# Two groups of x loads moved behind the first softmaxes of a Perceiver kernel

## The chip, the cores and the metric

The kernel runs on one core of one Trainium2 chip. The metric is the time on the device in microseconds (us), the median of several executions. Names used below: PE is TensorE, where "PEld" is its loading of weights; DVE is VectorE; ACT is ScalarE; POOL is GpSimd; SP is SyncE, which issues nearly all DMAs here. Each engine works through a queue of its own in order, and semaphores tie the queues together.

## The reference

A two-layer Perceiver step on x of 64 x 32 rows by 256 features, in float32. Each layer has cross attention into a context, self attention and a feed-forward part, each on a layer norm of x and added to x. The change lies in the first of the six, the cross attention of layer 0:

```python
def _L0_xattn_ref(q, latent_kv, Wq, Wkv_expand, Wout):      # 16 heads of 16
    qp = q @ Wq.T
    k, v = jnp.split(latent_kv @ Wkv_expand.T, 2, axis=-1)
    ...                                                     # split into heads
    scores = jnp.einsum('bhqd,bhkd->bhqk', qh, kh) * inv_sqrt_d
    scores = jnp.where(causal, scores, jnp.finfo(scores.dtype).min)
    attn = jax.nn.softmax(scores, axis=-1)
    out = jnp.einsum('bhqk,bhkd->bhqd', attn, vh)
    return out.transpose(0, 2, 1, 3).reshape(b, sq, H) @ Wout.T

x = x + _L0_xattn_ref(_layernorm(x, axis=-1), ctx_512, L0_xattn_Wq, L0_xattn_Wkv_expand, L0_xattn_Wout)
```

The causal mask lets 32 rows of a batch element see only its first 32 context rows, so only those are used here.

## The kernel before

The 2048 rows of x are 16 tiles of 128 rows (`NT`), `xs[0]` to `xs[15]`, which stay in SBUF through all six parts; four tiles make a group (`NG` = 4). A tile of x is 128 KB.

**Loads.** The program first issues all loads of its start on SP's queue: x of group 0 (L75), constants (L77), the weights `a_q` and `a_kv` (L86 to L96), the context of group 0 (`load_ctxa(0)`, L100 and L101), `a_o` (L105) and `vec` (L107); then x of the three other groups, twelve loads (L109), the context of groups 1 to 3, the rest of the constants (L112), and weights for later (L367, L372) with some tables (`cosN`, `sinN`, L669).

**The cross attention of layer 0** works by tiles in a software pipeline. For a group: `ln_group` or `norm` makes the layer norm, in the parts `stats` (L161, L162, DVE: BATCH_NORM_STATS2 and BATCH_NORM_AGGREGATE, each tile by itself), `ln_scale` for the whole group (POOL adds eps and raises to the power -1/2, L148 and L149; DVE makes the shift `lnh`, L176), and `ln_out` (L187, DVE, `xn_a`). `group(g, part)` turns the normalised rows (part 0, L226 and L230), makes the queries (part 1, L391 and L394) and the keys (part 2, L397; ACT spreads them into `kda`, L405).

For a tile: `score(t)` is 2 x 32 small matmuls into the PSUM tile `S_a` (L294), of which there is one; `softmax_rows` takes it out on DVE with scale and mask (`s_a`, L245), finds the maximum (`mx_a`, L254) and subtracts it on POOL (L255); `power(t)` is the exponential on ACT (L420); `share(t)` sums on DVE (`su_a`, L425), inverts (`ri_a`, L427) and multiplies on POOL (L428). `values(t)` makes the values on PE (`va`, L439) and masks them on DVE into `vda` (L449, four instructions). `heads_on_partitions(t)` turns the probabilities on PE (`ptp_a`, L263) and copies them on ACT (L265); `gather(t)` multiplies them with the values (`oa`, L464), and `project(t)` multiplies with `a_o` (`ya`, L493) and adds to x on DVE (L496). A step t of the loop holds, in this order on PE: the scores of t + 1, the projection of t - 2, the values of t + 1, the transpose of t, the gathering of t - 1, one part of the next group, and then the layer norm's part for the group after that (`norm(t // 4 + 2, t % 4, ...)`). Ahead of the loop, group 0 is normalised and made into queries and keys, tile 0 gets its scores, values and softmax, and group 1 is normalised.

**What sets the order.** PE's order is the order in which the program is written (a manual schedule). The queues of the other engines are filled by the tile framework's scheduler, which may move an instruction ahead of others once its operands can be there; loads on SP keep their order. So the order on DVE is not that of the text: in the built program DVE's instructions for the layer norm of groups 2 and 3 (written in the loop) stand ahead of the first tile's `s_a`.

**A column as a sign.** The kernel already holds back loads of weights for the next part (L482 to L487): POOL copies one column of a fresh result into the tile that is to be loaded, and the load, which overwrites it, must wait for that copy.

Of the kernel before, what the change touches and what calls it, by code (L numbers as in the profile page):

```python
# [13 lines left out]
P = 128  # L14
B, S, D = 64, 32, 256
NT = B * S // P
# [21 lines left out]
def bc(ap, axis, n):  # L38

    shape = list(ap.shape)  # L40
    shape.insert(axis, n)
    return ap.unsqueeze(axis).to_broadcast(shape)
# [3 lines left out]
def perceiver_kernel(ctx: ExitStack, tc: tile.TileContext, a: dict, out: bass.AP):  # L46
    nc = tc.nc
# [19 lines left out]
    def sm(name, shape):  # L67
        return small.tile(shape, F32, tag=name.split("_")[0], name=name)
# [4 lines left out]
    xs = [x[:, :D] for x in xf]  # L73
# [24 lines left out]
    def load_ctxa(g):  # L98
        src_ = a["ctxa"].rearrange("d (t c) -> d t c", c=P)[:, 4 * g : 4 * g + 4, :]
        nc.sync.dma_start(ctxa[0:DC, 4 * g : 4 * g + 4, :], src_)  # L100
        nc.sync.dma_start(ctxa[DC:P, 4 * g : 4 * g + 4, 0:64], src_[:, :, 64:P])  # L101
# [3 lines left out]
    nc.sync.dma_start(a_o, a["a_woT"].rearrange("(k p) o -> p k o", p=P))  # L105
    vec = const.tile([P, V_N], F32, name="vec")
    nc.sync.dma_start(vec, a["vecs"])  # L107
    for t in range(4, NT):
        nc.sync.dma_start(xs[t], a["x"][t * P : (t + 1) * P, :])  # L109
    for g in range(1, NG):  # L110
        load_ctxa(g)
    nc.sync.dma_start(cst[:, C_COST:], a["consts"][:, C_COST:])  # L112

    ident = cst[:, C_ID : C_ID + P]
# [244 lines left out]
    with tc.tile_pool(name="wA", bufs=2) as work, tc.tile_pool(  # L359
# [62 lines left out]
        def share(t):  # L422
            s = sc[t]
            su = sm(f"su_a{t}", [P, NH])
            nc.vector.tensor_reduce(su, s, AX.X, ALU.add)  # L425
            ri = sm(f"ri_a{t}", [P, NH])
            nc.vector.reciprocal(ri, su)  # L427
            nc.gpsimd.tensor_tensor(s, s, bc(ri, 2, S), ALU.mult)  # L428

        def values(t):  # L430

            vd = vals[t] = work.tile([P, 4, 4, 4, NH], F32, tag="vd", name=f"vda{t}", bufs=3)

            v_ps = [ps2.tile([P, 512], F32, tag="mm", name=f"va{t}_{z}") for z in range(2)]
            for jj in range(2):
                for z in range(2):
                    zs = slice(64 * z, 64 * z + 64)
                    for r in range(4):
                        nc.tensor.matmul(  # L439
                            v_ps[z][32 * r : 32 * r + 32, jj * D : (jj + 1) * D],  # L440
                            ctxa[zs, t, jj * S : (jj + 1) * S],
                            a_kv[zs, D : 2 * D],
                            start=True,
                            stop=True,
                            tile_position=(64 * z, 32 * r),
                        )
            for z in range(2):
                for jj in range(2):
                    nc.vector.tensor_tensor(  # L449
                        vd[:, 2 * z + jj],  # L450
                        v_ps[z][:, jj * D : (jj + 1) * D].rearrange(
                            "p (c h d) -> p c h d", c=4, h=4
                        ),
                        bc(bc(m4, 2, 16), 1, 4),
                        ALU.mult,
                    )
# [51 lines left out]
        values(0)  # L508
        power(0)
        share(0)  # L510
        lat[1] = ln_group(1, "a", power=True)

# [7 lines left out]
        for t in range(NT + 2):  # L520


            if t + 1 < NT:
                score(t + 1)
            if t > 1:
                project(t - 2)
            if t + 1 < NT:
                values(t + 1)
            if t < NT:
                turned[t] = heads_on_partitions(sc.pop(t), ps1, t, work, "a")  # L530
            if t + 1 < NT:
                power(t + 1)
            if 1 <= t <= NT:
                gather(t - 1)
            group(t // 4 + 1, (2, 0, 1, 3)[t % 4])
            norm(t // 4 + 2, t % 4, "a", mvs, lat)
            if t + 1 < NT:
                share(t + 1)
            for step in first.get(t, ()):
                step()  # L540
# [171 lines left out]
    with tc.tile_pool(name="wB", bufs=2) as work, tc.tile_pool(  # L712
# [237 lines left out]
        for t in range(NT + 1):  # L950
# [28 lines left out]
            if t < NT:  # L979
                share(t)  # L980
# [1054 lines left out]
```

## Time and profile before

| | us |
|---|---|
| median of 3 runs | 1284.66 |
| lowest and highest | 1284.02 and 1288.3 |
| profiled execution | 1288.21 |
| its span | 1286.4 |

Busy times of the profiled execution, out of its span:

| engine | busy us | share |
|---|---|---|
| PE | 1185.0 | 92% |
| PEld | 830.2 | 65% |
| DVE | 771.1 | 60% |
| ACT | 554.5 | 43% |
| POOL | 367.4 | 29% |

The mean granted clock of TensorE over the span was 0.941 of full speed. In a row of the timeline the first number is the start in us from the span's start, the second the length; then engine, line, operation, output<-input; in brackets stands how long the engine was idle before it and what ended that. A row that merges several instructions ends in their number (x4), and its length covers them all. "xcount" rows of stages give for each engine its busy time and in parentheses the number of instructions. A busy PE is not PE at its peak: its matmuls overlap.

### The profile page before, as it was taken

To read this page: it belongs to the slowest core of one execution; us is meant where nothing else is said; L and a number is where in the kernel's file an instruction comes from. 1 tells how busy PE (TensorE), PEld (TensorE's weight loads), DVE (VectorE), ACT (ScalarE), POOL (GpSimd) and SP (SyncE) were. 2 spreads that over 40 slices of the span, in tenths; PEclk is the share of its full clock that TensorE was granted. 3 is DMA by queue.
4 is the path that set the end of the run, shared out by engine and by line. 5 is a ranking of instruction groups with operands and counts; after the bars stand their busy time and mean duration, and the time that the engine had idled before them with its cause. 6 is when DMAs were issued, how large, how long until landed. Compare 5 with 4: busy or idle time off the path is not lost. (4 is left out here: it accounts for less than half of the span.)

```text
span 1286.4 us, 26074 instructions
## 1 busy us (share of the span) xinstructions
PE 1185.0 (92%) x10173; PEld 830.2 (65%) x10173; DVE 771.1 (60%) x1801; ACT 554.5 (43%) x1297; POOL 367.4 (29%) x438
## 2 busy tenths in 40 slices
PE   6999999999999998999889999999998798569997
PEld 4556767777776565776757667767765466436664
DVE  5666247778768875443287878776774564434333
ACT  2337354464544641213355646565564464311111
POOL 2333243455433621000154252010011354411111
PEclk8789999999999999989989989999999897669999
DMA  5021122343242423902263353111100344011110
GB/s 150 19 78 42 28 75 67 108 140 98 83 141 71 135 89 103 274 10 68 55 158 104 63 141 104 47 36 47 36 1 2 133 152 149 18 38 42 44 39 18
DMA packets 94971, 103.08 MB, mean 80 GB/s; under 512 B 37792, under 2 KB 71329, under 8 KB 94626
## 3 DMA queue, kind: packets, MB, share of 16 engines
q1 hardware_dynamic: 92978, 97.19, 26.4%
q0 software_dynamic: 1872, 4.23, 0.9%
q8 instruction: 81, 1.33, 0.4%
q14 instruction: 40, 0.33, 0.1%
HBM read 69.45 MB, written 32.85 MB: 80 GB/s over the span
## 5 line engine op out<-in xcount | busy, mean ns | idle before, releaser
L1348 ACT ACTIVATE pp<-Sd,nm 128x257 f32<-128x257 f32 x256 | 118.0, 474 | 77.1 <-DVE nm L1344 72.5
L761 PE MATMUL qb<-xT_b,b_q 128*128 128x256 f32 x512 | 123.4, 390 | 0.0
L761 PEld LDWEIGHTS qb<-xT_b,b_q 128*128 128x128 f32 x512 | 96.4, 193 | 39.9 <-issue 19.8
L852 PE MATMUL yb<-b_o,oTb 128*128 128x256 f32 x512 | 115.1, 384 | 0.0
L852 PEld LDWEIGHTS yb<-b_o,oTb 128*128 128x128 f32 x512 | 97.6, 192 | 14.0 <-issue 1.0
L1357 DVE TENSOR_TENSOR pp<-pp,rd 128x514 f32<-128x514 f32 x128 | 100.9, 789 | 2.1
L1344 DVE TENSOR_REDUCE nm<-Sd 128x2 f32<-128x514 f32 x128 | 82.9, 684 | 19.7 <-PE Sd L1336 19.6
L1379 ACT COPY pTd<-pt 128x512 f32<-128x512 f32 x112 | 61.5, 599 | 54.7 <-PE pt L1373 54.7
L1396 PE MATMUL od<-pTd,na 128*64 128x256 f32 x480 | 67.0, 401 | 11.2 <-issue 9.9
L780 POOL TENSOR_TENSOR q2b<-qTb 128x512 f32<-128x512 f32 x64 | 65.5, 1051 | 28.3 <-ACT qTb L769 17.0
L1336 PE MATMUL Sd<-ct,qTd 64*128 64x257 f32 x480 | 68.9, 404 | 0.7 <-ACT pp L1348 0.7
L769 ACT COPY qTb<-qb 128x512 f32<-128x512 f32 x64 | 37.4, 584 | 72.4 <-PE qb L761 70.8
L1373 PE MATMUL pt<-cst,pp 128*128 128x128 f32 x512 | 66.9, 274 | 0.0
L871 POOL TENSOR_TENSOR ynb<-ynb,vec 128x256 f32<-128x256 f32 x16 | 11.6, 724 | 188.4 <-DVE ynb L870 188.4
L1373 PEld LDWEIGHTS pt<-cst,pp 128*128 128x128 f32 x512 | 58.9, 141 | 9.8 <-issue 5.4
L1134 PE MATMUL qd<-xT_d,d_m 128*128 128x256 f32 x256 | 64.1, 393 | 0.2 <-ACT xT_d L230 0.2
L814 DVE RECIPROCAL rqb<-rqb 128x512 f32<-128x512 f32 x16 | 53.5, 3342 | 17.8 <-ACT rqb L809 17.8
L1412 PE MATMUL yd<-d_n,co 128*128 128x256 f32 x256 | 63.2, 403 | 0.0
L643 PE MATMUL yc<-c,hc 128*128 128x256 f32 x256 | 59.2, 387 | 2.7 <-DVE hc L638 2.7
L1910 POOL DMA_INDIRECT out_dram<-os,ti x23 | 22.6, 984 | 126.0 <-DVE os L1907 103.1
L1412 PEld LDWEIGHTS yd<-d_n,co 128*128 128x128 f32 x256 | 50.0, 200 | 13.4 <-issue 6.5
L1134 PEld LDWEIGHTS qd<-xT_d,d_m 128*128 128x128 f32 x256 | 46.6, 191 | 16.9 <-issue 6.4
(371 smaller groups left out, 2376.6 us busy)
## 6 DMA issues: line engine op xcount, KB each, us to landing
srt<-pad SPq DMA_DIRECT2D x17, 1040.0 KB
mb<-maskd SPq DMA_DIRECT2D x64, 128.0 KB
ct<-ctd SPq DMA_DIRECT2D x30, 257.0 KB
rct<-in_ctxT_dram SPq DMA_DIRECT2D x32, 128.5 KB
rrt<-in_ctxT_dram SPq DMA_DIRECT2D x64, 64.2 KB
ctd<-rct SPq DMA_DIRECT2D x32, 128.5 KB
nad<-rna SPq DMA_DIRECT2D x16, 256.0 KB
fw<-in_f_wg_dram SPq DMA_DIRECT2D x8, 512.0 KB
```

The costliest lines, as they stand in the source:

```text
L761: nc.tensor.matmul(q_ps[:, hh, :], b_q[:, k, h * P : (h + 1) * P], xT[:, k, c0 : c0 + 256], start=(k == 0), stop=(k == KC - 1),)
L780: nc.gpsimd.tensor_tensor(q2[:, 4 * h4 : 4 * h4 + 4, :], q, q, ALU.mult)
L852: nc.tensor.matmul(y_ps, oT[:, h, :], b_o[:, h, :], start=(h == 0), stop=(h == NH - 1))
L1134: nc.tensor.matmul(q_ps[:, r, :], m[:, k, pr * P : (pr + 1) * P], xT[:, k, c0 : c0 + 256], start=(k == 0), stop=(k == KC - 1),)
L1336: nc.tensor.matmul(s_ps[:, hh, :NKV], qT[hs, b % 8, 4 * u : 4 * u + 4, :], ct[hs, b % 4, :], start=True, stop=True,)
L1344: nc.vector.tensor_reduce(nm, s_ps[:, :, :NKV], AX.X, ALU.max, negate=True)
L1348: nc.scalar.activation(pp[:, hh, :], s_ps[:, hh, :NKV], AF.Exp, bias=nm[:, hh : hh + 1], accum_out=sd[:, hh : hh + 1],)
L1357: nc.vector.tensor_tensor(pp, pp, bc(rd, 2, NKV), ALU.mult)
L1373: nc.tensor.transpose(pt[:, hh * 256 + u * P : hh * 256 + u * P + P], probs[b][:, u, hh, c * P : (c + 1) * P], ident,)
L1379: nc.scalar.copy(pT[:, c, :], pt)
L1396: nc.tensor.matmul(o_ps[64 * hh : 64 * hh + 64, 0, :], na[:, j, c, :], pT[:, c, hh * 256 : (hh + 1) * 256], start=(c == 0), stop=(c == 1),)
L1412: nc.tensor.matmul(y_ps, co[:, pr, :], n[:, pr, :], start=(pr == 0), stop=False)
```

## The change

x of group 1 (tiles 4 to 7) is loaded where it was. The eight loads for groups 2 and 3 leave that place. A new function `load_x(g, sign)` copies the first column of `sign` into the first column of each of the group's four x tiles on POOL and issues the tile's load behind it; `share(t)` calls it for t = 0 and t = 1 with the sums `su` of that tile, for groups 2 and 3.

```diff
-    for t in range(4, NT):
+    for t in range(4, 8):
         nc.sync.dma_start(xs[t], a["x"][t * P : (t + 1) * P, :])
     for g in range(1, NG):
         load_ctxa(g)
+
+    def load_x(g, sign):
+
+        for t in range(4 * g, 4 * g + 4):
+            nc.gpsimd.tensor_copy(xs[t][:, 0:1], sign[:, 0:1])
+            nc.sync.dma_start(xs[t], a["x"][t * P : (t + 1) * P, :])
+
     nc.sync.dma_start(cst[:, C_COST:], a["consts"][:, C_COST:])
...
             ri = sm(f"ri_a{t}", [P, NH])
             nc.vector.reciprocal(ri, su)
             nc.gpsimd.tensor_tensor(s, s, bc(ri, 2, S), ALU.mult)
+            if t < 2:
+                load_x(2 + t, su)
```

The lines below L112 move down by 7, those from L429 on by 9. In the built program PE's and ACT's queues hold the same instructions in the same order. POOL has its copies ahead of the multiplication by `ri` of the same tile. On DVE the stats of group 2 stand behind the second tile's `vda`, and those of group 3 are spread over the third and fourth tile.

## The prediction

> **What bounds the kernel now.** The page comes first: PE is busy 92% of the span, so only what lets PE wait, or slows its clock, can be worth much. Then the waits of PE over the first 120 us, longest first (waiter, what released it, total us, times, longest):
>
> ```profile
> PE S_a L294 <- DVE s_a L245: 5.9, 1, 5.9
> PE oa L464 <- DVE x L496: 1.5, 1, 1.5
> PE qa L391 <- DVE vda L449: 1.3, 2, 1.0
> PE ptp_a L263 <- POOL s_a L428: 1.1, 1, 1.1
> ```
>
> One wait stands out: the second tile's scores want the PSUM tile that `s_a` (L245) of the first tile must empty. The timeline says why that is late. PE first, then DVE between the two scores (start, length, what):
>
> ```profile
> 19.59 1.19 PE L439 MATMUL va<-a_kv,ctxa 64*32 64x256 f32 x32
> 26.68 1.10 PE L294 MATMUL S_a<-kda,qTa 32*32 32x64 f32 x64 [5.89 <-DVE s_a L245]
> ...
> 31.85 1.12 PE L263 MATMUL ptp_a<-cst,s_a 128*128 128x128 f32 x4 [1.11 <-POOL s_a L428]
> 32.90 3.77 PE L397 MATMUL ka<-ctxa,a_kv 64*128 64x512 f32 x4
> ```
> ```profile
> 18.55 1.67 DVE L187 SCALAR_TENSOR_TENSOR xn_a<-x,lnr_a,lnh_a 128x256 f32<-128x256 f32 x4
> 20.14 0.74 DVE L161 BATCH_NORM_STATS2 lnb_a<-x 128x6 f32<-128x256 f32 x2
> ...
> 23.22 0.16 DVE L176 SCALAR_TENSOR_TENSOR lnh_a<-lnm_a,lnr_a 128x4 f32<-128x4 f32 x1 [1.16 <-POOL lnr_a L149]
> ...
> 25.86 0.16 DVE L176 SCALAR_TENSOR_TENSOR lnh_a<-lnm_a,lnr_a 128x4 f32<-128x4 f32 x1 [1.47 <-POOL lnr_a L149]
> 25.94 0.68 DVE L245 SCALAR_TENSOR_TENSOR s_a<-S_a,caus 128x512 f32<-128x512 f32 x1
> ```
>
> The scores of tile 0 were complete by 19.67 (26.68 is tile 1). DVE was free of group 1's `xn_a` at 20.22, yet took `s_a` at 25.94: it first normalised groups 2 and 3, whose x had landed and which stand ahead in its queue, including two waits (1.16, 1.47) for POOL's power.
>
> Last, stages (length, PE, PEld, DVE, ACT, POOL busy, granted clock, DMA share, GB/s):
>
> ```profile
> 20.80:26.60 5.80, 0.00 (x0) 0.00 (x0) 3.17 (x16) 0.00 (x0) 2.53 (x4) 0.86 0.63 174
> 26.60:31.80 5.20, 3.69 (x96) 1.89 (x96) 4.67 (x13) 0.63 (x1) 2.09 (x3) 0.50 0.08 14
> 31.80:45.40 13.60, 13.55 (x207) 8.24 (x212) 6.35 (x16) 6.32 (x11) 3.55 (x4) 0.50 0.01 2
> ```
>
> The gap costs twice: 5.8 us of nothing, then 20 us at half clock, of which 13.6 us (31.8 to 45.4) have PE saturated. Before 31.8 the chain is DVE, POOL and ACT (PE 3.69 of 5.20), so the clock matters little there.
>
> **The change, part by part.** The built order of the changed kernel has PE and ACT as they were. On DVE the 18 instructions of groups 2 and 3 (8 stats, 8 aggregates, 2 `lnh`) leave the place ahead of the first `s_a`: group 2's stats stand behind tile 1's four `vda`, group 3's are spread through tiles 2 and 3. SP loses eight x loads from between x[7] and the `ctxa` loads, and issues them behind `sinN`. POOL gains 2 x 4 copies of one column, ahead of the multiplication by `ri` of tiles 0 and 1, and its two powers move back.
>
> 1. *DVE ahead of the first softmax.* `s_a` follows `xn_a` directly, which ends at 20.22; one aggregate (0.17, at 18.36) also goes from ahead of `xn_a`, so about 20.12. 25.94 - 20.12 = **-5.8**. S(1) would start at 26.68 - 5.8 = 20.9, hard behind `va` (ends 20.78). Everything down to tile 0's transpose (`ptp_a`, now 31.85) hangs on this DVE/POOL/ACT chain and moves with it, to 26.05.
>
> 2. *POOL copies.* Row: a POOL COPY of 128x1 took 181 to 184 ns (L482, 4 of them). Four are 0.72. Tile 0: `su` ends at 29.85 and the multiplication starts at 30.75 behind `ri`, 0.9 for the copies to fit in; bounds 0 and +0.5, if each costs 0.35 with its start. I take **+0.1**; it lies on the path, as `ptp_a` waits for that multiplication. Tile 1: 34.61 - 34.19 leaves 0.42, so about 0.4 late; the work that hides it is PE's `ka`, S(2) and `va`, since `ptp_a`(1) came at 39.89, 4.2 after its input at 35.66. Uncovered it would cost 0.4.
>
> 3. *SP and the loads.* SP issued an x load every 0.43 to 0.47 us. Eight fewer bring the later ones about 3.7 forward: `sinN` is issued by 23.4 instead of 27.15, so SP stands ready when the first copies end (su(0) at 29.85 - 5.8 = 24.05, plus the copies: 24.3 to 24.8). Behind these waits on SP stands only `b_q`, wanted from 59 on. x[8] landed at best as x[0] did (issue 0.73, stats at 2.88: 2.15) and at worst as x[4] under a full queue (10.90 to 14.16: 3.26). DMA carried 174 GB/s in the gap and 14 after 26.6; a megabyte less ahead of it drains some 3 us sooner. I take 2.2: x[8] at 26.7, x[11] at 28.0. DVE gets to x[8]'s stats behind `vda`(1), which ends at 32.48 - 5.8 = 26.7. Queued behind them on DVE are `su`(1) and `ri`(1), for which POOL and then `ptp_a`(1) wait. Four stats (0.40 to 0.43) and aggregates (0.18) are 2.3; DVE idled 1.01 ahead of `su`(1) and 3.34 ahead of `s_a`(2), so they fit. `ri`(1) comes about 0.6 late, under the 4.2 of item 2. **0**; even 3 us of later landing costs nothing while PE is slow there.
>
> 4. *Group 3's stats.* Tile 2's is covered by DVE's 0.41 before `vda`. At tile 3 DVE is the bound (no idle from 44.16 to 51.2): two stats and two aggregates enter ahead of `vda`(3), 2 x 0.43 + 2 x 0.16 = 1.18, and tile 0's second normalisation (0.43 + 0.18) moves behind it: +0.57. `oa` and `qa` wait for DVE there already (0.29 and 0.28), so PE is late by **+0.57**. The rest (1.5) falls into 3.61 of DVE idle before `s_a`(4). The second power waits on POOL in an idle of 4 us. Bounds 0 and +1.2.
>
> 5. *The clock.* At full speed `va`(1) would end near 23.8 (its second half waits for `vda`(0), 28.67 - 5.8, plus 0.8), and `ptp_a` starts at 26.15: a gap of 2.35 remains. Windows of 3.41 us, cut where the clock changed in this trace:
>
> ```profile
> 18.14:21.56 3.42, 1.89 (x96) 1.16 (x96) 3.27 (x12) 1.06 (x2) 0.10 (x1) 1.00 0.71 198
> 21.56:24.97 3.41, 0.00 (x0) 0.00 (x0) 1.67 (x10) 0.00 (x0) 1.68 (x4) 1.00 0.58 151
> ...
> 72.76:76.17 3.41, 1.93 (x52) 1.40 (x36) 2.53 (x6) 0.14 (x1) 2.22 (x3) 1.00 0.09 36
> 76.17:79.58 3.41, 2.40 (x9) 1.22 (x6) 2.51 (x8) 1.24 (x3) 0.93 (x2) 0.50 0.21 52
> ```
>    The clock fell after 21.56 to 24.97 with PE at 0.00, but also after 72.76 to 76.17 with PE busy 1.93, whose longest gap was 1.49; it did not after 18.14 to 21.56 with 1.89. In the changed kernel the same cut gives about 0.34 + 0.27 + 0.82 = 1.4 in 21.56 to 24.97, all small tiles. The Trainium skill (TensorE: Matmul & The Clock Gate, "Why this matters for your kernels") says the clock holds as long as no gap exceeds about 3 us. By that rule 2.35 is harmless, the clock stays full, and 31.85 to 44.69 shrinks: PE's pieces at their full-speed rows are 0.66 + 1.98 + 0.85 + 1.09 + 0.66 + 1.12 + 1.09 = 7.45, about 8.4 with `va` waiting for ACT's `kda`, against 12.84: a further -4.4. By the row a gap of 1.49 sufficed. I follow the row: it falls anyway, but at a window's end between 24.7 and 28.1 rather than before S(1). Work done at full clock between 26.15 and that moment saves its own length; over evenly spread cuts (1.95 squared / 2) / 3.41 = **-0.56**. It rises again, as now, behind the transposes of group 1. Bounds: -4.4 (no fall) and +1.7 (the rise comes one window later, at half speed).
>
> Sum: -5.8 + 0.1 + 0.57 - 0.56 = **-5.7**. Nothing behind layer 0's cross attention has an absolute time (every later load hangs on a tile), so the shift should last. The profiled execution took 1288.2 (span 1286.4, 1.8 around it) and would take 1282.5; it is 3.5 above the median, 1284.66, which becomes **1279.0**.
>
> **The rivals.**
> - *The clock stays up.* For it: 18.14 to 21.56 held at 1.89, and a cut near 24.5 splits the gap in two. Against: 1.93 fell. -5.8 + 0.1 + 0.57 - 4.4 = about -9.6: 1275.
> - *Little is left.* The 1.5 us `qa` and `oa` gaps near 75 and 77 show that DVE decides later tiles too: with +1.2 from item 4, +0.5 from item 2 and a late rise (+1.7), -2.4: 1282, no measurable change.
> - *The change doesn't do what it says.* The column could hold back only the load and not DVE; but the built order shows `s_a` ahead of all moved stats. Little chance, included in the former.
> - *Slower: the loads are late.* DVE takes its queue in order, so x[8]'s stats hold up `su`(1). `su`(1) may wait until 31.9 before `ptp_a`(1) (39.89 - 5.8 = 34.1, less 0.69 + 0.4 + 1.05) is late, 3.8 after my 28.1. Beyond that each us costs one, and the change turns to loss where loads land 3.8 + 5.7 = 9.5 later than taken, 11.7 after issue; at 13 it gives 1286, and with the 0.3% to show, 1289 at 16. The longest landing seen there, 3.26, speaks against.
>
> **How the numbers follow.** Within 0.3% (3.9 us, about what a measurement of this kernel tells from no change) means above 1280.8. Likeliest 0.63 (own range 1277 to 1281, by the clock's cuts and items 2 and 4); clock stays 0.15; little left 0.17; loads late 0.05. The likeliest lies 1.8 inside the bound and keeps nearly all its chance there: faster 0.78, same 0.18, slower 0.04. The range reaches from just below the second case, 1274, to beyond the third, 1283.
>
> **What would show it.** Right: S(1) near 20.9 with no wait for `s_a`; the clock falling between 24.7 and 28.1 and back near 40; x loads issued from about 24.5 and no DVE wait for them over 0.5 us; a PE wait at `qa` of tile 3 near 0.85. Wrong: DVE waiting for x ahead of `su`(1), `ptp_a`(0) later than 26.5, or a full clock throughout (then 1275).

## The result

| | before | changed |
|---|---|---|
| median of 20 runs each, us | 1289.51 | 1283.14 |
| profiled execution, us | 1288.21 | 1285.48 |
| its span, us | 1286.4 | 1283.7 |

The ratio of the changed kernel to the one before is 0.9958, with a 95% interval of 0.9938 to 0.9979. On 1289.5 that is 5.4 us saved, with an interval of 2.7 to 8.0: faster. The two medians lie 6.4 apart, inside that interval. One of the 20 runs of the kernel before took 2896.2, which the ratio leaves out. The median of the kernel before is now 1289.51, where the first three runs had given 1284.66. A forecast of 1279.0 with a range of 1274 to 1283 was made from the latter, and the measured 1283.14 lies 0.14 above that range.

Read the changed kernel's profile in the same order as before. Of the waits of PE over the first 120 us (waiter, what released it, total us, times, longest), the first line of before, 5.9 us for `s_a`, is gone, and no other wait took its length:

```profile
PE oa L473 <- DVE x L505: 2.2, 2, 1.5
PE ptp_a L270 <- POOL s_a L435: 2.0, 1, 2.0
...
PE qa L398 <- DVE vda L458: 1.0, 1, 1.0
```

PE's timeline shows tile 1's scores directly behind `va`, without a wait in brackets, and a gap of 1.98 ahead of the first transpose:

```profile
19.66 1.19 PE L448 MATMUL va<-a_kv,ctxa 64*32 64x256 f32 x32
20.78 0.85 PE L301 MATMUL S_a<-kda,qTa 32*32 32x64 f32 x64
...
25.86 1.12 PE L270 MATMUL ptp_a<-cst,s_a 128*128 128x128 f32 x4 [1.98 <-POOL s_a L435]
```

DVE's timeline shows why. `s_a` follows group 1's `xn_a` at once, at 19.94 (before: 25.94). The first stats of group 2 come at 26.41 and show no wait for their load; nor does `su` behind them wait for a load, but for ACT's exponential:

```profile
18.35 1.67 DVE L194 SCALAR_TENSOR_TENSOR xn_a<-x,lnr_a,lnh_a 128x256 f32<-128x256 f32 x4
19.94 0.68 DVE L252 SCALAR_TENSOR_TENSOR s_a<-S_a,caus 128x512 f32<-128x512 f32 x1
...
26.41 0.77 DVE L168 BATCH_NORM_STATS2 lnb_a<-x 128x6 f32<-128x256 f32 x2
...
27.51 0.69 DVE L432 TENSOR_REDUCE su_a<-s_a 128x16 f32<-128x512 f32 x1 [0.25 <-ACT s_a L427]
```

The added work on POOL, the four copies of tile 0, took 0.54 and ended before the multiplication behind them had its input; it still waited 0.30 for `ri`:

```profile
23.92 0.54 POOL L116 COPY x<-su_a 128x1 f32<-128x1 f32 x4 [1.45 <-DVE su_a L432]
24.76 1.05 POOL L435 TENSOR_TENSOR s_a<-s_a,ri_a 128x512 f32<-128x512 f32 x1 [0.30 <-DVE ri_a L434]
```

Last, the stages, cut where the clock changed (length, PE, PEld, DVE, ACT, POOL busy, granted clock, DMA share, GB/s). The clock fell all the same, at 25.1, but came back at 35.3, where it had come back at 45.4 before:

```profile
18.20:21.61 3.41, 2.66 (x160) 1.84 (x160) 3.27 (x9) 1.08 (x2) 0.19 (x1) 1.00 0.78 226
21.61:25.10 3.49, 1.75 (x34) 0.84 (x32) 2.99 (x9) 0.63 (x1) 1.74 (x6) 1.00 0.08 13
25.10:35.30 10.20, 9.44 (x116) 4.58 (x116) 7.31 (x24) 4.47 (x8) 5.58 (x10) 0.50 0.36 107
35.30:45.50 10.20, 9.42 (x181) 6.36 (x180) 8.39 (x24) 3.75 (x8) 3.20 (x4) 1.00 0.01 2
```

In this pair of profiles the scores of tile 5 start at 51.02 instead of 58.22, which is 7.2 earlier, though the spans differ by only 2.7. Where the rest went, and whether 7.2 is the change's own, the repeats below settle.

### The profile page after: what moved, and what is told of

The parts are those of the page before. It is cut to its first block, busy times and chain, and to the rows that moved or that the text cites. A ratio compares the mean times of both kernels' runs of the same rounds, so it can differ in the third digit from the quotient of the medians.

```text
span 1283.7 us, 26087 instructions
## 1 busy us (share of the span) xinstructions
PE 1183.7 (92%) x10173; PEld 828.5 (65%) x10173; DVE 769.9 (60%) x1801; ACT 555.3 (43%) x1297; POOL 368.2 (29%) x446
## 3 DMA queue, kind: packets, MB, share of 16 engines
q1 hardware_dynamic: 92978, 97.19, 26.1%
## 5 line engine op out<-in xcount | busy, mean ns | idle before, releaser
L770 PEld LDWEIGHTS qb<-xT_b,b_q 128*128 128x128 f32 x512 | 97.4, 195 | 41.4 <-issue 20.9
L652 PEld LDWEIGHTS yc<-c,hc 128*128 128x128 f32 x256 | 50.3, 199 | 12.6 <-DVE hc L647 3.5
L1143 PEld LDWEIGHTS qd<-xT_d,d_m 128*128 128x128 f32 x256 | 47.1, 193 | 17.1 <-issue 6.4
```

The costliest lines, as they stand in the source:

```text
L652: nc.tensor.matmul(y_ps, hs[f][:, i * P : (i + 1) * P], c_2[:, f, :], start=(f == 0), stop=(f == 7),)
L770: nc.tensor.matmul(q_ps[:, hh, :], b_q[:, k, h * P : (h + 1) * P], xT[:, k, c0 : c0 + 256], start=(k == 0), stop=(k == KC - 1),)
L1143: nc.tensor.matmul(q_ps[:, r, :], m[:, k, pr * P : (pr + 1) * P], xT[:, k, c0 : c0 + 256], start=(k == 0), stop=(k == KC - 1),)
```

## The experiments

The theory, which the prediction's first step states: the gain is the DVE work that no longer stands ahead of `s_a` of tile 0. "S(n)" below is the start of the scores of tile n on PE. Totals are medians, and ratios are against the kernel before, run on the same chip beside them. Its median there was 1289.22 (69 runs) for the kernels with the stats held back, without the column, and with matmuls added to the one or the other kernel; 1290.41 (11 runs) for those with group 3 alone or by tile 3's sums and the first repeats; and 1291.26 (11 runs) for that with tile 2's sums and the second repeats. The last kernel's is given with it.

### Is it the order on DVE, or the relief of the DMA queues?

The kernel before with its loads where they were, early. The stats of groups 2 and 3 are held back by a zero, made of the first and second tile's sums, that is added to one column of x:

```diff
+            if t < 2:
+                z = sm(f"zc_a{t}", [P, 1])
+                nc.gpsimd.tensor_scalar(z, su[:, 0:1], 0.0, None, ALU.mult)
+                for u in range(8 + 4 * t, 12 + 4 * t):
+                    nc.gpsimd.tensor_tensor(xs[u][:, 0:1], xs[u][:, 0:1], z, ALU.add)
```

> Loads where the kernel before has them; only the stats of groups 2 and 3 are held back, by a zero made from tile 0's or tile 1's sums and added to one column of each x tile on POOL (exact, x unchanged). Theory (the place on DVE is all of it): s_a of tile 0 near 20.0, scores of tile 1 near 20.9, scores of tile 5 near 51.4 us (after: 51.02, before: 58.22; POOL has five small operations instead of four copies, up to 0.5 us late at the first transpose), total 5 to 6 us below before. Rival (fewer loads ahead, so earlier data and less DMA traffic, makes the gain): scores of tile 1 at 26.7 as before, no gain.

Measured: 1282.86, ratio 0.9938 (0.9914 to 0.9962). `s_a` came at 20.21 and S(5) at 51.59, in an execution that took 1288.85 as a whole. DVE's timeline and PE's read like those of the changed kernel:

```profile
18.62 1.67 DVE L187 SCALAR_TENSOR_TENSOR xn_a<-x,lnr_a,lnh_a 128x256 f32<-128x256 f32 x4
20.21 0.68 DVE L245 SCALAR_TENSOR_TENSOR s_a<-S_a,caus 128x512 f32<-128x512 f32 x1
```

```profile
21.02 0.85 PE L294 MATMUL S_a<-kda,qTa 32*32 32x64 f32 x64
...
26.22 1.11 PE L263 MATMUL ptp_a<-cst,s_a 128*128 128x128 f32 x4 [2.08 <-POOL s_a L428]
```

So the whole gain is there with every load left early. No part of it that could be told apart comes from the relief of the queues.

### Is the column needed?

The changed kernel without the copies; the loads stand at the same place of the program, with nothing that they wait for:

```diff
     def load_x(g, sign):
         for t in range(4 * g, 4 * g + 4):
-            nc.gpsimd.tensor_copy(xs[t][:, 0:1], sign[:, 0:1])
             nc.sync.dma_start(xs[t], a["x"][t * P : (t + 1) * P, :])
```

> The eight loads stand behind the tables on SP as in the changed kernel, but without the column, so nothing holds them or the stats back. In the built order one stat of x[8] then stands ahead of tile 0's vda. Theory (what waits ahead of the first softmax on DVE sets the time): s_a of tile 0 near 20.0, but vda only when x[8] lands, issued near 22.7 and landed near 25.0, so su of tile 0 some 3 us later than in the changed kernel, first transpose near 29, scores of tile 5 near 54, total 2 to 3 us below before. Rival (a later place of the loads suffices): scores of tile 5 at 51, 5 to 6 us below before.

Measured: 1283.37, ratio 0.9957 (0.9936 to 0.9979). The expectation misplaced the loads: they went out ahead of the tables, from 18.26 to 23.0, and not behind them. DVE's timeline:

```profile
18.42 1.67 DVE L193 SCALAR_TENSOR_TENSOR xn_a<-x,lnr_a,lnh_a 128x256 f32<-128x256 f32 x4
21.32 0.69 DVE L251 SCALAR_TENSOR_TENSOR s_a<-S_a,caus 128x512 f32<-128x512 f32 x1 [1.23 <-PE S_a L300]
...
22.65 0.42 DVE L167 BATCH_NORM_STATS2 lnb_a<-x 128x6 f32<-128x256 f32 x1
```

`s_a` again stands directly behind `xn_a`. That it came only at 21.32 is PE's doing in this execution (1.23 of waiting for the scores, the second half of which began at 20.74 instead of 19.33). S(5) was at 51.15, and no time that can be told apart was lost. So the column is not needed either: a later place of the loads in the program is enough for the scheduler to put these stats behind `s_a` (one of them still ahead of tile 0's `vda`).

### Does the gain grow with the DVE work that is moved?

Only group 3 held back; group 2 loaded early again:

```diff
-    for t in range(4, 8):
+    for t in range(4, 12):
...
-            if t < 2:
-                load_x(2 + t, su)
+            if t == 1:
+                load_x(3, su)
```

> Only group 3 is held back (by tile 1's sums); x of group 2 is loaded in its old place, and its stats, its shift and their wait for POOL's power stay ahead of the first softmax. Theory (the gain is the length of DVE work and waiting ahead of s_a): s_a of tile 0 near 23.3 (before 25.94, after 19.94), scores of tile 1 near 24.1, a gap on PE of 3.3 us, the clock falls before 28, scores of tile 5 near 55.5 (up to 1.7 either way by the clock's windows). Rival (all or nothing, as the gap's clock cost stays or goes whole): scores of tile 5 within 1 us of 58.2 or of 51.0.

DVE's timeline now has one group's stats, and one wait for POOL's power, ahead of `s_a`:

```profile
20.29 0.74 DVE L168 BATCH_NORM_STATS2 lnb_a<-x 128x6 f32<-128x256 f32 x2
...
23.11 0.16 DVE L183 SCALAR_TENSOR_TENSOR lnh_a<-lnm_a,lnr_a 128x4 f32<-128x4 f32 x1 [1.47 <-POOL lnr_a L156]
23.19 0.68 DVE L252 SCALAR_TENSOR_TENSOR s_a<-S_a,caus 128x512 f32<-128x512 f32 x1
```

23.19 lies between 19.94 (none ahead) and 25.94 (both ahead), and was expected at 23.3. S(1) came at 23.93 behind a wait of 0.90, and S(5) at 54.32, where 55.5 with 1.7 to either side was expected. One execution took 1285.7. The start of tile 1 follows the DVE work ahead of it group by group.

### What is the clock worth with the DVE work left where it was?

The kernel before with matmuls that nobody reads in PE's two gaps: ten behind the values of tile 0, four ahead of its transpose. It does more work, and leaves nothing out.

```diff
         values(0)
+        fill = ps1.tile([P, 256], F32, tag="PT", name="fill0")
+        for _ in range(10):
+            nc.tensor.matmul(fill, ident, cst[:, 0:256], start=True, stop=True)
...
+            if t == 0:
+                fill = ps1.tile([P, 256], F32, tag="PT", name="fill1")
+                for _ in range(4):
+                    nc.tensor.matmul(fill, ident, cst[:, 0:256], start=True, stop=True)
             if t < NT:
                 turned[t] = heads_on_partitions(sc.pop(t), ps1, t, work, "a")
```

> The kernel before, with PE kept busy in its two gaps by matmuls that nobody reads: 10 behind the first tile's values and 4 ahead of the first transpose (128x128 by 128x256, 0.53 us each at full clock). The 5.8 us of waiting stay, the half clock behind them should not come. Theory (the gap costs twice, the clock part 4.4 us by the sum of PE's pieces): clock full from 20 to 60 us, scores of tile 1 at 26.7, of tile 3 near 40.5 (before 44.69), of tile 5 near 54 (before 58.22), total about 4 us below before. Rival (DVE, POOL and ACT bound this stretch too, the clock is worth little): scores of tile 5 later than 57, total within 1 us.

The granted clock was full from 23.5 to 110, after 3.4 us at half. In PE's timeline each of these matmuls counts as two:

```profile
22.64 4.95 PE L511 MATMUL fill<-cst 128*128 128x256 f32 x20
27.52 0.85 PE L294 MATMUL S_a<-kda,qTa 32*32 32x64 f32 x64
...
53.89 0.85 PE L294 MATMUL S_a<-kda,qTa 32*32 32x64 f32 x64
```

S(1) is 0.8 later than in the mean of before (26.75), because it now stands behind the unread matmuls and not behind `s_a` (from 26.17 on). Yet S(5) is at 53.89 as expected, 4.3 ahead of the first profile of before and 3.3 ahead of the mean of three. So the clock alone is worth 3 to 4 us in this stage. The total was 1287.94, ratio 0.9990 (0.9965 to 1.0014): from the total a gain of the stage's size can't be told from none.

### Can the changed kernel keep its clock?

The changed kernel with only the four unread matmuls ahead of the first transpose (the second half of the diff above).

> The changed kernel, with 4 such matmuls in the gap of 2.0 us ahead of the first transpose. Theory (a gap of 2.0 us is what makes the clock fall at 25): clock full from 20 to 60 us, first transpose near 26.0, scores of tile 3 near 34.5 (after 37.18), of tile 5 near 48 (after 51.02), total 3 us below the changed kernel and 8 to 9 below before. Rival (in 25 to 35 us the changed kernel is bound by DVE and POOL, or the fill itself is in the way): scores of tile 5 at 50.5 or later, total as the changed kernel.

Measured: 1280.76 (16 runs), ratio 0.9940 (0.9915 to 0.9966). The clock no longer fell at 25. It did not fall between 24 and 34 in any of the five kernels with these matmuls (1.99 us) in that gap, one above and three below, and it fell between 25 and 28 in all five profiles with the first `s_a` moved up and without them. But S(3) came at 37.25 and S(7) at 64.00, no earlier than in the changed kernel (37.18, 62.98), as the rival had it. DVE's timeline says why:

```profile
31.97 0.16 DVE L183 SCALAR_TENSOR_TENSOR lnh_a<-lnm_a,lnr_a 128x4 f32<-128x4 f32 x1 [1.93 <-POOL lnr_a L156]
32.05 0.42 DVE L168 BATCH_NORM_STATS2 lnb_a<-x 128x6 f32<-128x256 f32 x1
...
32.91 0.67 DVE L252 SCALAR_TENSOR_TENSOR s_a<-S_a,caus 128x512 f32<-128x512 f32 x1
```

PE's timeline shows what followed:

```profile
35.38 1.94 PE L233 MATMUL tp_a<-cst,xn_a 128*128 128x128 f32 x8 [1.66 <-DVE vda L458]
```

Tile 2's softmax stands in the same kind of queue as tile 0's had: behind a wait for POOL's power (1.93) and two stats of a group that is not needed yet. PE waited 1.66, and its clock fell there instead, at 35. In the changed kernel DVE's order is another:

```profile
31.82 0.69 DVE L252 SCALAR_TENSOR_TENSOR s_a<-S_a,caus 128x512 f32<-128x512 f32 x1 [2.47 <-PE S_a L301]
32.43 0.15 DVE L183 SCALAR_TENSOR_TENSOR lnh_a<-lnm_a,lnr_a 128x4 f32<-128x4 f32 x1
```

There `s_a` stands ahead of the shift `lnh` and of the stats. So the four matmuls on PE changed more than the clock: with them in the program, the scheduler filled DVE's queue differently. What a full clock is worth with DVE's order left as it is in the changed kernel was not run.

### And with group 3 still later?

Two versions of the last kernel hold group 3 behind a later tile's sums, tile 3's or tile 2's.

```diff
-            if t < 2:
-                load_x(2 + t, su)
+            if t in (0, 3):
+                load_x(2 + (t > 0), su)
```

> The changed kernel with the 4 unread matmuls ahead of the first transpose, and group 3 held back by tile 3's sums instead of tile 1's: in the built order its stats then stand in DVE's idle time behind tile 3's ri, and none ahead of tile 2's or tile 3's softmax. Theory (with the clock full, the first fill run was held up at 33 to 35 us by two more stats that had slipped ahead of s_a of tile 2, and by its shift's wait for POOL's power): s_a of tile 2 near 32.3 instead of 32.9, clock full from 20 to 60, scores of tile 3 near 36, of tile 5 near 48.5 (changed kernel 51.02), total 2 to 3 us below the changed kernel. Rival (DVE and POOL bound this part at full clock, so the fill brings nothing): scores of tile 5 at 50.5 or later, total equal to the changed kernel within 1 us.

Tile 3's sums: 1282.34 (6 runs), ratio 0.9914 (0.9888 to 0.9941). The clock stayed full to 70.5. `s_a` of tile 2 came at 31.93, still behind `lnh` and its wait of 1.93 but with no stats ahead of it, and S(5) at 49.55, which is 1.5 ahead of the changed kernel. Then the load was late, and DVE waited for x[12] with the next softmax behind it:

```profile
44.58 0.43 DVE L168 BATCH_NORM_STATS2 lnb_a<-x 128x6 f32<-128x256 f32 x1 [2.04 <-DMA x<-in_x_dram]
```

S(7) was at 63.24 (changed kernel: 62.98). The 1.5 were given back within two tiles.

```diff
-            if t < 2:
-                load_x(2 + t, su)
+            if t in (0, 2):
+                load_x(2 + (t > 0), su)
```

> The changed kernel with the 4 unread matmuls, and group 3 held back by tile 2's sums: its x lands earlier than with tile 3's, so DVE should not wait for it, but one of its stats stands ahead of tile 3's maximum and two more ahead of tile 3's vda. Theory (whoever stands ahead of the next softmax on DVE is paid for): no DVE wait for x, scores of tile 5 near 50.6 (1 us later than with tile 3's sums, 49.55), scores of tile 7 near 57.5 as both others, total 2 us below the changed kernel. Rival (with the clock full, these stats find idle time): scores of tile 5 at 49.6 and of tile 7 at 56 or earlier.

Tile 2's sums: 1279.69 (6 runs), ratio 0.9921 (0.9893 to 0.9950). The clock was full from 23.5 to 126, and S(3) came at 35.83. But again a load was late, against the expectation, here inside tile 3's softmax. DVE's timeline:

```profile
37.94 0.69 DVE L252 SCALAR_TENSOR_TENSOR s_a<-S_a,caus 128x512 f32<-128x512 f32 x1
40.04 0.43 DVE L168 BATCH_NORM_STATS2 lnb_a<-x 128x6 f32<-128x256 f32 x1 [1.41 <-DMA x<-in_x_dram]
40.38 0.67 DVE L261 TENSOR_REDUCE mx_a<-s_a 128x16 f32<-128x512 f32 x1
```

PE then waited 1.78 ahead of `oa`, S(5) was at 51.32, and S(7) at 63.27, again as in the changed kernel. (The expectation's 57.5 for tile 7 is the start of tile 6, here 57.74.) From S(3) to S(7) it took 27.44, against 25.80 there. Two causes are left for that: the late load, or the length of the stats on a DVE that is the bound at full clock.

### The same without a late load

As the last kernel (group 3 by tile 2's sums, four unread matmuls), but with all loads early and only the stats held back, as in the first experiment, against which the diff stands (the four matmuls come on top):

```diff
-            if t < 2:
+            if t in (0, 2):
                 z = sm(f"zc_a{t}", [P, 1])
                 nc.gpsimd.tensor_scalar(z, su[:, 0:1], 0.0, None, ALU.mult)
-                for u in range(8 + 4 * t, 12 + 4 * t):
+                for u in range(8 + 2 * t, 12 + 2 * t):
                     nc.gpsimd.tensor_tensor(xs[u][:, 0:1], xs[u][:, 0:1], z, ALU.add)
```

> The last kernel (four unread matmuls ahead of the first transpose, group 3 by tile 2's sums) with all loads left early, so that only the stats are held back, by a zero made of the sums and added to one column of x. There DVE waited 1.41 for x of group 3 at 40.04, ahead of tile 3's maximum, and the time from S(3) to S(7) was 27.44, against 25.80 in the changed kernel. Theory: that late load is what gave the clock's gain back. Then DVE waits for no load, S(3) is near 35.8, S(3) to S(7) takes 25.8 to 26.3, and S(7) comes at 61.6 to 62.1, 1.2 to 1.7 ahead of the mean of the changed kernel's profiles (63.34). Rival: the stats' own length on DVE does it, with or without the load. Then S(3) to S(7) takes about 27.4 and S(7) comes near 63.3 again. Total by the theory 1.2 to 1.7 below the changed kernel, some 1281.5 to 1282 beside a kernel before of 1289.5; by the rival as the changed kernel, near 1283.5. The totals alone will hardly tell these apart; the starts will.

Measured: 1279.34 (14 runs) beside 1290.94 (19), ratio 0.9918 (0.9889 to 0.9947). In DVE's timeline of tile 3 the same instructions, in a slightly different order, now follow each other without a wait:

```profile
38.17 0.42 DVE L161 BATCH_NORM_STATS2 lnb_a<-x 128x6 f32<-128x256 f32 x1
38.51 0.68 DVE L245 SCALAR_TENSOR_TENSOR s_a<-S_a,caus 128x512 f32<-128x512 f32 x1
39.10 0.41 DVE L501 TENSOR_TENSOR x<-x,ya 128x256 f32<-128x256 f32 x1
39.43 0.68 DVE L254 TENSOR_REDUCE mx_a<-s_a 128x16 f32<-128x512 f32 x1
```

S(3) was at 36.05 and S(7) at 62.00: 25.95 between them, as the theory had it. The late load it was. S(7) is 1.34 ahead of the mean of the changed kernel's profiles (63.34), although in this execution the first scores ran at half clock and S(1) came only at 22.82. Counted from S(1), S(7) took 39.18 here and 42.15 to 42.48 in the changed kernel. So about 3 us more can be had after the change. They belong to three things together: the four matmuls with the full clock, group 3's stats a tile later, and its loads early. Later stats without the matmuls were not run, and `lnh` with its wait of 1.93 still stands ahead of tile 2's `s_a`. This version has the lowest ratio but one, and the best stage; its interval still overlaps that of the changed kernel (0.9938 to 0.9979) from 0.9938 to 0.9947, so that it beats it is likely by the totals, not shown.

### How much of a difference of two profiles is chance?

Each of the two kernels once more, unchanged, twice:

> The kernel before, unchanged, profiled once more. Theory (what spreads the runs is TensorE's clock in the parts behind, whose falls depend on how an execution meets windows of 3.41 us): scores of tile 1 within 0.5 us of 26.7 and scores of tile 5 within 2 us of 58.2, but the span anywhere between 1278 and 1297, and longer by about half of what it has more of half clock than the first profile (150 us). Rival (the early part varies itself): scores of tile 5 off by more than 3 us.

> The changed kernel, unchanged, profiled once more. Theory: scores of tile 1 within 0.5 us of 20.8, of tile 5 within 2 us of 51.0, the span anywhere between 1273 and 1292, with its half clock time beside it (143 us in the first profile). Rival: the 7 us at tile 5 are this one execution's luck, and the repeat shows tile 5 later than 54.

> The kernel before, profiled a third time. Theory (the early gain is 5 to 7 us on the mean, 5.85 between the two pairs so far, the spread of single executions is the clock's): scores of tile 1 at 26.7, of tile 5 between 56 and 60. Rival (the second profile, 56.3, is the usual case and the gain nearer to 4.5): 55.5 to 56.8.

> The changed kernel, profiled a third time. Theory: scores of tile 1 within 0.5 us of 20.9, of tile 5 between 50 and 52.5, the clock falling between 24.7 and 28.1 in this execution too. Rival (in some executions the gap before the first transpose does not cost the clock): no fall before 60 us and scores of tile 5 at 48.5 or earlier.

The repeats took 1289.95 and 1290.97 (before), and 1290.03 and 1276.14 (changed). The starts from all profiles of the two kernels ("transpose" is the first one, `ptp_a` of tile 0; "half clock" is from the fall between 20.9 and 26.1 to the next rise):

| us | before | | | changed | | | difference of means |
|---|---|---|---|---|---|---|---|
| S(1) | 26.68 | 26.72 | 26.85 | 20.78 | 21.29 | 21.11 | -5.69 |
| transpose | 31.85 | 31.91 | 32.03 | 25.86 | 26.48 | 26.29 | -5.72 |
| S(3) | 44.69 | 42.45 | 43.30 | 37.18 | 37.96 | 37.45 | -5.95 |
| S(5) | 58.22 | 56.30 | 57.15 | 51.02 | 51.81 | 51.30 | -5.85 |
| S(7) | 70.18 | 68.25 | 69.11 | 62.98 | 63.77 | 63.26 | -5.84 |
| half clock lasted | 20.5 | 17.1 | 20.5 | 10.2 | 10.2 | 10.2 | |
| span | 1286.4 | 1288.2 | 1289.2 | 1283.7 | 1288.3 | 1274.4 | |

The first pair's 7.2 was 1.35 too much by chance: at tile 5 the first profile of before was that kernel's latest of three, and the first of the changed kernel its earliest. The rest of the program adds far more chance than the stage has effect. The starts of the same instructions, compared along two traces, show it. Against the first profile of before, its first repeat stood at -1.9 at 67 us, -6.2 from 145 to 440, +1.2 at 550, about +4.0 from 800 to 930, and +1.7 at the end, with nothing changed. The first pair of before and changed stood at -7.4 from 200 to 400, -4.3 from 405, +2.2 at 580 and -2.7 at the end. One such step, in the stages of the kernel before:

```profile
393.50:400.50 7.00, 5.58 (x33) 3.10 (x31) 6.45 (x17) 3.90 (x9) 0.00 (x0) 1.00 0.16 36
```

and in those of the changed kernel:

```profile
393.50:400.50 7.00, 6.30 (x18) 3.99 (x19) 5.79 (x8) 1.54 (x3) 5.44 (x6) 0.52 0.46 153
```

Here the clock fell in the one execution and not in the other (1.00 against 0.52), and 3 of the 7.4 us were gone. The repeats show steps of that size in both directions for the same kernel. The first repeats' expectation, that a span is longer by half of what it has more of half clock, did not hold: the repeat of before had 146 us of it against 152 and was 1.8 longer, that of the changed kernel 143 against 146 and was 4.6 longer. What else spreads the executions stays open. So the loss of the first pair's gain needs no mechanism of the change; and the last profile of the changed kernel, 12.1 ahead of the first of before at its end, is no evidence for more.

## Why the prediction was right and wrong

**What failed is the last step of its sum**: that the profiled execution "is 3.5 above the median, 1284.66, which becomes 1279.0". 1284.66 was a median of three runs. With 20 runs the kernel before has 1289.51, and with 69 others 1289.22. Half of those 69 lie between 1286.6 and 1292.5, and of medians of three drawn from them only about 9 in 100 come out at 1284.66 or less. The profiled 1288.21 was close to typical and not 3.5 above. With the right start the same sum gives 1289.5 - 5.7 = 1283.8, where 1283.14 was measured. The range allowed for the size of the saving and nothing for the start: the three runs spread over 4.3 us, and that should have widened it upwards.

**The saving** was predicted as 5.7. The totals say 5.4 (2.7 to 8.0), and three profiles of each kernel say 5.85 at tile 5. By the steps:

1. *DVE ahead of the first softmax*, -5.8: `s_a` was predicted at 20.12 and came at 19.94, S(1) was predicted at 20.9 and came at 20.78 without a wait (21.11 with a wait of 0.25 in the second repeat), and in the mean of three S(1) moved by -5.69. Right, and shown to be the cause: the same move without any moved load gives the same (51.59 at tile 5), and half of it gives a part (54.32).
2. *POOL copies*, +0.1 for tile 0: 0.54 instead of 0.72, and 0 on the path, as the wait of 0.30 for `ri` shows. The transpose was predicted at 26.05 with 0.1 more for this, and came at 25.86; in the mean of three it moved by -5.72. Tile 1's copies pushed its multiplication back, to 28.89, and no PE wait followed from it.
3. *SP and loads*, 0: right. x was issued from 24.12 (predicted 24.3 to 24.8), and no stats waited for it. The slower rival, in which late loads hold DVE, did not happen here. Its mechanism exists: 2.04 us in the version with tile 3's sums.
4. *Group 3 at tile 3*, +0.57: mis-sized. From S(3) to S(5) both kernels take 13.85 where the clock is full at S(3), as in both repeats of each; over the three pairs the term is +0.10. DVE's timeline of before, in its first repeat:

```profile
44.70 0.68 DVE L245 SCALAR_TENSOR_TENSOR s_a<-S_a,caus 128x512 f32<-128x512 f32 x1
45.41 0.69 DVE L254 TENSOR_REDUCE mx_a<-s_a 128x16 f32<-128x512 f32 x1
46.01 0.41 DVE L496 TENSOR_TENSOR x<-x,ya 128x256 f32<-128x256 f32 x1
46.46 0.43 DVE L161 BATCH_NORM_STATS2 lnb_b<-x 128x6 f32<-128x256 f32 x1
46.92 0.18 DVE L162 BATCH_NORM_AGGREGATE lnm_b<-lnb_b 128x2 f32<-128x6 f32 x1
47.02 1.39 DVE L449 TENSOR_TENSOR vda<-va,cst 128x256 f32<-128x256 f32 x4
```

   and of the changed kernel:

```profile
39.42 0.68 DVE L252 SCALAR_TENSOR_TENSOR s_a<-S_a,caus 128x512 f32<-128x512 f32 x1
40.02 0.16 DVE L169 BATCH_NORM_AGGREGATE lnm_a<-lnb_a 128x2 f32<-128x6 f32 x1
40.11 0.39 DVE L168 BATCH_NORM_STATS2 lnb_a<-x 128x6 f32<-128x256 f32 x1
40.42 0.66 DVE L261 TENSOR_REDUCE mx_a<-s_a 128x16 f32<-128x512 f32 x1
41.01 0.40 DVE L505 TENSOR_TENSOR x<-x,ya 128x256 f32<-128x256 f32 x1
41.34 0.17 DVE L169 BATCH_NORM_AGGREGATE lnm_a<-lnb_a 128x2 f32<-128x6 f32 x1
41.43 0.39 DVE L168 BATCH_NORM_STATS2 lnb_a<-x 128x6 f32<-128x256 f32 x1
41.74 1.39 DVE L458 TENSOR_TENSOR vda<-va,cst 128x256 f32<-128x256 f32 x4
```

   From the start of `s_a` to that of `vda` it is 2.32 in both. Two pairs of a stat and an aggregate came in and one went out. From `s_a` to `mx` it is 0.71 without and 1.00 with a pair between them, so 0.29 for 0.16 + 0.39 by the rows. From the addition to x to `vda` it is 0.73 with the other new pair, and was 1.01 with the old one, whose stat takes the x that was just written. The 0.28 saved there makes up for the 0.29. Adding up row lengths missed that. PE's waits moved accordingly: `oa` 0.76 instead of 0.50 in that repeat, and `qa`'s 0.29 is gone; the single wait near 0.85 at `qa` that was predicted isn't there.
5. *The clock*, -0.56: it fell at 25 to 26 in all three profiles of the changed kernel, within the predicted 24.7 to 28.1, and came back at 35 to 36.5, not near 40. Between the transpose and S(3) the saving grew by only 0.23 in the mean, for -0.56 predicted. This term was mis-sized by a third of a microsecond the other way than item 4, and that the two errors nearly cancelled is luck. Nor was it the gap of 5.9 that brought the half clock in every execution of before: in the second repeat the clock fell at 20.9, ahead of the gap.

**Row against rule.** The prediction weighed the rule that it takes from the Trainium skill (TensorE: Matmul & The Clock Gate, "Why this matters for your kernels"), by which the clock holds as long as no gap exceeds about 3 us (then -4.4 more), against a row in which it fell with a longest gap of 1.49. The row was right: the clock fell inside gaps of 1.98 and 1.99 in three profiles of three, and inside one of 2.08 with the loads left early. Filling that gap removed the fall there. The stretch from the transpose to S(3), which the -4.4 prices at 8.4 instead of 12.84, took 7.85 in the kernel before with unread matmuls. In the changed kernel it took 10.62 with the four matmuls alone, because the order of DVE that was built with them held up tile 2's softmax, and 8.41 to 8.85 with group 3's stats later. So the price of the stretch was about right, but 12.84 was the longest of three profiles (10.54 and 11.27 in the repeats): from the mean of the three it is about -3, not -4.4.

**The bound of 0.3%.** Faster was given 0.78, and the ratio 0.9958 is on that side, though its interval reaches to 0.9979.

## What to carry to other kernels

Data that lands early invites a scheduler to put work on it ahead of work that the critical engine waits for; look in an in-order queue for what stands between an input's arrival and the instruction that takes it, and if it isn't due yet, place its load (or another operand) later. When single executions differ by more than the effect, judge the mechanism by start times inside its own stage over several profiles, and the total by many runs, the baseline's above all: three runs misplaced it by nearly the whole effect. And when something is added to one engine's queue, look again at the order that the scheduler gives the others: four matmuls on PE put other work ahead of a softmax on DVE.

## What the runs showed of the hardware

In each of the fourteen traces all changes of the granted clock lie whole steps of 3.41 us apart: in the first profile of before at 24.9, 45.4, 76.1 and 83.0, that is 6, 9 and 2 steps. Where the steps lie against the program differs by execution. In the kernel before the fall came between 20.9 and 24.9 and lasted 5 or 6 steps, in the changed kernel between 25.1 and 26.1 and lasted 3.

In six of the fourteen traces, the second repeat of before among them, the clock fell already between 20.0 and 21.1, ahead of the gaps that this document is about. In the step that ended there PE was busy for 2.2 to 2.4 of the 3.41 us, and no gap in it was longer than 0.75. Over the first 140 us each of the 30 falls ended a step with at most 2.36 us busy. But steps with less (down to 1.72) also passed without a fall, and in the changed kernel the clock fell at 540.5 although PE's rows show no idle from 537.1 on (`t1p`, on tiles of 64*96). So neither the longest gap nor the busy time tells by itself when the clock falls.

In the changed kernel, 1.99 us of extra matmuls in a gap of 2 us were enough to keep the clock full there. Why it came back after 10.2 us in the changed kernel and took up to 20.5 before, with PE saturated for the last 13.6 of them, was not tried.
